# Back from the frequencies: the loads of the inverse transform in one run of 4 KB for each partition

## The chip, the cores and the metric

The kernel runs on one core of a Trainium2 chip. The metric is the device time of one execution, in microseconds; lower is better. The core has TensorE (PE) for matmuls, VectorE (DVE), ScalarE (ACT), GpSimd (POOL) and SyncE (SP), each with its own queue of instructions that it works through in order, and 16 DMA engines, which move data for all of them. In this kernel SP and ACT issue nearly all transfers, each on a queue of its own. SBUF is the memory of 128 partitions that the engines compute on, PSUM the one that TensorE writes, DRAM the large one outside.

## The reference

Two layers on an image `x` of 4 x 56 x 56 positions with 128 channels:

```
layer 0:  x = x + proj(7x7 neighbourhood attention(layernorm(x)))
          x = x + fc2(gelu(fc1(layernorm(x))))
layer 1:  t = x as 3136 tokens
          t = t + q * sum over tokens(k * v)              # of layernorm(t)
          t = t + gated mix of four STU branches          # of u = layernorm(t)
          branch i sees the first T/(1,2,4,8) tokens:
            U+ = irfft(rfft(phi) * rfft(u))               # 16 filters, causal
            U- = the same of u with every other sign turned
            out = U+ . M_phi_plus[i] + U- . M_phi_minus[i] + three lags of u . M_u[i]
```

The long convolution with its 16 filters is what the kernel does by transforms: tokens to frequencies, a 128 x 128 matrix product at every frequency, and frequencies back to tokens.

## The kernel before

All is float32. The program has four stages, one after the other.

1. Attention of the four images, with the dense work of the image before filled in between by a list of costs (`run`, `dense`). Its order is written out by hand.
2. The rest of the last image, while the matrices `M_phi` are weighted into `mc` (`matrices`). Its loads, `mat`, are 512 KB each: 128 partitions, one run of 4 KB in each.
3. The frequencies. There are R = 245 of them in each of two halves (`yd[0]` and `yd[1]`, sum and difference). `make` builds the matrices of eight frequencies at a time, `product` multiplies, and L1077 stores the result to `yd` in DRAM, which is laid out frequency x slot and token group x channel. A frequency has 128 rows of 128 channels, 64 KB.
4. The way back. The tokens are in four parts of N = 784 each, worked in two pairs (`pair`), and each part in L = 98 positions by eight phases. For each pair the odd half of the spectrum (`par` 1) gives the four odd phases, the even half (`par` 0) the four even ones. Since the frequencies stand on the partitions, 245 of them take two parts (`fh` 0 and 1): by `RT = (0, 128, R)` the first has 128 rows and the second 117.

What stage four does in turn, and on which engine:

- `fetch_back(pair, par, fh)` (L1088 to L1099) loads a part from `yd` to a tile of the ring on SP's queue. A row of the ring holds eight runs of 4 KB (a run is two token parts x four images x 128 channels), which in DRAM lie 8 KB apart, the other pair's between them. A load of 128 rows is one transfer. For 117 rows there are two: 112 rows, the largest multiple of 16, and 5 rows.
- `io` and `ie` (L1103, L1219) are the cosine and sine tables of the inverse transform, loaded on ACT's queue.
- `odd` and `even` are butterflies in place on VectorE (L1137, L1138).
- `products` runs the matmuls on TensorE (L1176): first all phases with `fh` 0, then all with `fh` 1, accumulating in eight PSUM banks. Then VectorE adds each bank to `xo` (L1188), the residual, which L1225 has loaded from `xd`: 98 partitions, four images of 4 KB in each. ACT's queue stores `xo` to the output (L1192).

The ring has two tiles, one for each `fh`, with room for both halves of the spectrum. A load for the second pair can begin when TensorE has read what stood there.

Stage three and four are ordered by the scheduler of the language, which reorders transfers on SP's queue by its own estimate. The order on SP's queue around the change is, before: first ring load (`par` 1, `fh` 0), two stores of `yd`, second ring load (`par` 0, `fh` 0), the last four stores of `yd`, then the second parts, `xo`, and the four loads of the second pair.

The inverse tables are computed on the host with zeros in the rows beyond 117, and `products` cuts the table to the rows of the data (`it[: z.shape[0]]`).

Of the kernel before, what the change touches and what calls it, by code (L numbers as in the profile page):

```python
# [9 lines left out]
FP = mybir.dt.float32  # L10
# [6 lines left out]
B, H, W, C = 4, 56, 56, 128  # L17
# [23 lines left out]
PH = 8  # L41
L = N // PH
R = NF // PH
RT = (0, 128, R)
SLOTS = (0, 6, 4, 2, 1, 7, 5, 3)
BACK = ((0, 2, 4, 6), (1, 5), (3, 7))
FC = 8
# [9 lines left out]
def conv_attn_hybrid_kernel(ctx: ExitStack, tc: tile.TileContext, a: dict, out: bass.AP):  # L57
    nc = tc.nc

    cpool = ctx.enter_context(tc.tile_pool(name="const", bufs=1))  # L60
    dram = ctx.enter_context(tc.tile_pool(name="scratch", bufs=1, space=DRAM))
    xd = dram.tile([B, T, C], FP, name="xd")
    ud = dram.tile([NP, B, C, NCH * CW], FP, name="ud")
    pd = dram.tile([2 * NK, NCH * CW], FP, name="pd")
    yd = dram.tile([2, R, C, C], FP, name="yd")

    front = ExitStack()
    fp = front.enter_context(tc.tile_pool(name="front", bufs=1))
# [895 lines left out]
    with tc.tile_pool(name="last", bufs=1, side="right") as own, tc.tile_pool(  # L964
        name="weigh", bufs=1, side="right"
# [14 lines left out]
    with tc.tile_pool(name="w3", bufs=2) as wp, tc.tile_pool(  # L980
        name="ps_g", bufs=6, space=PSUM
# [64 lines left out]
        def product(c, part):  # L1046

            v, g = spectra[c], made[c]
            f0 = part // 4 * 4
            h, last = part // 2 % 2, min(many[c], f0 + 4)  # L1050
            if part % 2 == 0:
                sums[0] = ps_y.tile([C, 4, C], FP, tag="y", name=f"py_{c}_{part}")
            py, f1 = sums[0], f0 + part % 2 * 2
            for f in range(f1, min(f1 + 2, last)):
                for r in range(2):
                    for m in range(4):
                        slot = SLOTS.index(4 * h + m)
                        nc.tensor.matmul(  # L1058
                            py[32 * m : 32 * m + 32, f - f0, :],
                            weights(v, 1 - r, f, slot),  # L1060
                            g[:, (2 * slot + r) * FC + f, :],
                            start=(r == 0),
                            stop=(r == 1),
                        )
            if part % 2 == 0:
                return

            k = last - f0
            if h == 0:
                sums[1] = wp.tile([C, 4, C], FP, tag="ya", name=f"ya_{c}_{part}", bufs=1)  # L1070
                nc.scalar.copy(sums[1][:, :k], py[:, :k])
                return
            for i, op in enumerate((ALU.add, ALU.subtract)):
                ys = wp.tile([C, 4, C], FP, tag=f"ys{i}", name=f"ys_{c}_{part}_{i}")
                nc.vector.tensor_tensor(ys[:, :k], sums[1][:, :k], py[:, :k], op)  # L1075
                at = FC * c + f0
                nc.sync.dma_start(yd[i, at : at + k].rearrange("f q e -> q f e"), ys[:, :k])  # L1077

# [1 line left out]
        PAIR = 2 * B * C  # L1082
# [3 lines left out]
            ring.append(gpool.tile([C, 2, 4, 2, PAIR], FP, tag="g", name=name))  # L1086

        def fetch_back(pair, par, fh):  # L1088
            f0, n = RT[fh], RT[fh + 1] - RT[fh]
            y = ring[fh][:, 1 - par]  # L1090
            for r0, r1 in ((0, n // 16 * 16), (n // 16 * 16, n)):
                if r0 < r1:
                    nc.sync.dma_start(
                        y[r0:r1].rearrange("f m s x -> f (m s) x"),
                        yd[par, f0 + r0 : f0 + r1].rearrange("f (k n) e -> f k (n e)", k=8)[
                            :, :, PAIR * pair : PAIR * (pair + 1)
                        ],
                    )
            return y[:n].rearrange("f m s (j x) -> f j m s x", j=2)  # L1099

        def odd_waves(pool, pair, fh):
            t = pool.tile([C, 32 * L], FP, tag="io", name=f"io_{pair}_{fh}")
# [27 lines left out]
    with tc.tile_pool(name="w4", bufs=1) as wp, tc.tile_pool(  # L1130
        name="ps_t", bufs=8, space=PSUM
# [34 lines left out]
        def products(pair, phases, terms, xos, dst):  # L1166


            banks = {}
            for fh in range(2):  # L1170
                for j, p, *what in phases:
                    if fh == 0:
                        banks[j, p] = ps_t.tile([L, B, C], FP, tag="t", name=f"pi_{pair}_{j}_{p}")
                    of = terms(fh, j, *what)
                    for k, (it, z) in enumerate(of):
                        nc.tensor.matmul(  # L1176
                            banks[j, p],
                            it[: z.shape[0]],
                            z,
                            start=(fh == 0 and k == 0),  # L1180
                            stop=(fh == 1 and k == len(of) - 1),
                        )
                    yield
                    if fh == 0:
                        continue
                    xo = xos[j][:, :, p, :]
                    o = 2 * pair + j
                    nc.vector.scalar_tensor_tensor(  # L1188
                        xo, banks[j, p], on[:L, o : o + 1], xo, ALU.mult, ALU.add
                    )  # L1190
                    if dst and p == 6:
                        nc.scalar.dma_start(dst[j], xos[j].rearrange("n b p e -> n b (p e)"))  # L1192
# [6 lines left out]
        for pair in range(2):  # L1199
            here, into = (  # L1200
                [
                    d[:, N * o : N * (o + 1)].rearrange("b (n p) e -> n b (p e)", p=PH)
                    for o in (2 * pair, 2 * pair + 1)
                ]
                for d in (xd, tokens_out)
            )
            ys, xos = {}, []
            ios = [
                waves_back[0] if pair == 0 else odd_waves(wpool, pair, 0),
                odd_waves(wp, pair, 1),  # L1210
            ]
            ys[1, 0] = fetch_back(pair, 1, 0) if pair else ready[1]
            ys[1, 1] = fetch_back(pair, 1, 1)
            ies = []

            def even_loads():
                for fh in range(2):
                    t = wp.tile([C, 16 * L], FP, tag=f"ie{fh}", name=f"ie_{pair}_{fh}")
                    nc.scalar.dma_start(t, a["itab_even"][pair, fh])  # L1219
                    ies.append(t.rearrange("f (j p r n) -> f j p r n", j=2, p=4, r=2))  # L1220
                ys[0, 0] = fetch_back(pair, 0, 0) if pair else ready[0]
                ys[0, 1] = fetch_back(pair, 0, 1)
                for j in range(2):
                    xo = wp.tile([L, B, PH, C], FP, tag=f"xo{j}", name=f"xo_{pair}_{j}")
                    nc.sync.dma_start(xo.rearrange("n b p e -> n b (p e)"), here[j])  # L1225
                    xos.append(xo)

            if pair == 0:
                even_loads()
            for par, step, phases in ((1, odd, odd_phases), (0, even, even_phases)):  # L1230
                zs = {}
                for fh in range(2):
                    for j in range(2):
                        zs[fh, j] = step(ys[par, fh][:, j])
                        for _ in range(4):
                            next(behind, None)
                for _ in behind:
                    pass
                if par and pair:
                    even_loads()  # L1240

                def terms(fh, j, *what, zs=zs, ios=ios, ies=ies):
                    if len(what) > 1:
                        kind, i = what
                        return [
                            (ios[fh][:, j, kind, m, r, i], zs[fh, j][kind][2 * m + r])
                            for m in range(2)
                            for r in range(2)
                        ]
                    return [(ies[fh][:, j, what[0], r], zs[fh, j][what[0]][r]) for r in range(2)]  # L1250

                behind = products(pair, phases, terms, xos, None if par else into)
# [7 lines left out]
def _laid_out(inputs):  # L1260
# [8 lines left out]
    x = a["x"].reshape(B, NG, GR, NQ, QC, C)  # L1269
    a["x"] = x.transpose(0, 5, 1, 3, 2, 4).reshape(B, C, NG, GT)  # L1270

    r, c, kr, kc = np.ix_(range(GR), range(QC), range(KR), range(KC))
    i, j = kr - r, kc - c
    inside = (i >= 0) & (i < WIN) & (j >= 0) & (j < WIN)
    at = np.where(inside, i * WIN + j, 0)
# [39 lines left out]
    for name, kinds, m in (("itab_even", BACK[:1], 1), ("itab_odd", BACK[1:], 2)):  # L1315
        inv = np.zeros((NP // 2, 2, C, 2, len(kinds), m, 2, len(kinds[0]), L))
        for k, ps in enumerate(kinds):

            of = both[:, :, ps, :, :m].reshape(NP // 2, 2, L, len(ps), 2, m, R)
            for i in range(2):  # L1320
                part = of[..., RT[i] : RT[i + 1]].transpose(0, 6, 1, 5, 4, 3, 2)
                if m == 1:
                    part = part.transpose(0, 1, 2, 3, 5, 4, 6).reshape(
                        NP // 2, -1, 2, 1, 2, len(ps), L
                    )
                inv[:, i, : part.shape[1], :, k] = part
        a[name] = inv.reshape(NP // 2, 2, C, -1).astype(np.float32)

    turn = 2 * np.pi / PH * np.outer(np.arange(PH), SLOTS)
# [29 lines left out]
```

## Time and profile before

| | us |
|---|---|
| median of 3 runs | 2086.72 (2086.64 to 2090.88) |
| the profiled execution's own time | 2095.97 |
| its span, first to last instruction | 2094.2 |
| TensorE busy over the span | 1896.0 (91%) |
| VectorE, ScalarE, GpSimd busy | 1230.1, 1000.9, 854.7 |
| way back, first ring load issued to the end of the span | 1857.9 to 2094.2 |
| TensorE busy from 1858 to 2094 | 183.4 of 236.0 |
| ring loads | 8 of 4096 or 3584 KB, 4 of 160 KB |
| `xo` loads, `out` stores | 4 each, 1568 KB |
| `io`, `ie` loads | 4 of 1568 KB, 4 of 784 KB |

The profile shows one execution. In a line of a group or of the timeline, `128*98 128x512` is a matmul whose weights have 128 rows and 98 columns and whose output is 512 wide; `x64` counts instructions. A float32 matmul of the program is two instructions here. `issue` is time in which an engine waited for nothing that the profile shows. Start times are from the span's start.

### The profile page before, as it was taken

The page shows a single profiled execution, that of the slowest core. Times are in us where ns is not written, and L with a number is a line of the kernel's source. Part 1 is how long each engine was busy: PE and PEld are TensorE (multiplying, and loading weights), DVE is VectorE, ACT ScalarE, POOL GpSimd, SP SyncE. Part 2 cuts the span into 40 slices and gives each one's busy share as a digit, 9 for nine tenths or more (in the row PEclk, how much of TensorE's full clock was granted, in tenths as well). Part 3 has the DMA queues.
Part 4 walks back from the last instruction along what each step waited for, and adds up shares of the span by engine and source line. Part 5 has one row for each costly group of instructions (what it writes and reads, how often), then busy time and mean ns, then how long its engine had stood idle before and what let it go on. Part 6 is the DMA issues. An engine that isn't in the chain of part 4 may idle for free.

```text
span 2094.2 us, 56418 instructions
## 1 busy us (share of the span) xinstructions
PE 1896.0 (91%) x23878; PEld 1201.0 (57%) x23878; DVE 1230.1 (59%) x2636; ACT 1000.9 (48%) x2199; POOL 854.7 (41%) x1272
## 2 busy tenths in 40 slices
PE   6899999998998989999999876999999999978896
PEld 3565554564554654554654334888888888852332
DVE  3777545555445555445655742677766766655566
ACT  2466675554675555765553331555555555530000
POOL 2233222462122562113740151777777777730000
PEclk8899999998999999999999986999999999988998
DMA  3130000242000450000445364344444444369993
GB/s 109 35 122 11 1 1 1 94 152 93 1 1 1 141 172 25 1 1 14 165 160 168 114 227 120 104 129 129 124 120 129 129 124 124 98 224 270 229 276 100
DMA packets 189989, 221.95 MB, mean 106 GB/s; under 512 B 10964, under 2 KB 170005, under 8 KB 187144
## 3 DMA queue, kind: packets, MB, share of 16 engines
q1 hardware_dynamic: 181596, 165.24, 28.0%
q0 software_dynamic: 2752, 34.33, 4.2%
q10 hardware_dynamic: 5388, 18.76, 2.8%
q8 instruction: 188, 3.08, 0.6%
q14 instruction: 65, 0.53, 0.1%
HBM read 140.33 MB, written 77.97 MB: 104 GB/s over the span
## 4 chain that ended last, share of the span: by engine, by line
PE 68%; DMA 9%; issue 7%; DVE 5%; ACT 4%; SPq 3%; POOL 2%; another core or an unknown queue 0%; ACTq 0%; DVEq 0%; POOLq 0%
PE pg L1027 14%; PE py L1058 12%; PE ppt L761 5%; PE px L658 4%; PE ph L511 3%; DMA xo<-xd 3%; PE pf L502 3%; PE pl L710 3%; PE pi L1176 3%; PE par L602 2%; DMA ring<-yd 2%; PE pav L807 2%; PE pv L788 2%; DMA tab<-in_tab 2%; ACT p L737 2%
## 5 line engine op out<-in xcount | busy, mean ns | idle before, releaser
L750 POOL TENSOR_SCALAR p<-p,den 112x280 f32<-112x280 f32 x448 | 216.2, 503 | 558.9 <-DVE den L748 291.7
L1040 DVE COPY g<-pg 128x512 f32<-128x512 f32 x496 | 320.1, 689 | 186.8 <-PE pg L1027 186.8
L1038 ACT COPY g<-pg 128x512 f32<-128x512 f32 x496 | 271.1, 602 | 263.9 <-PE pg L1027 263.9
L1027 PE MATMUL pg<-ph,mc 32*128 32x128 f32 x7936 | 308.1, 288 | 26.8 <-DMA ph<-pd 15.5
L1027 PEld LDWEIGHTS pg<-ph,mc 32*128 32x128 f32 x7936 | 257.5, 190 | 70.4 <-issue 57.8
L737 ACT ACTIVATE p<-p,low 112x280 f32<-112x280 f32 x448 | 231.2, 517 | 135.5 <-DVE low L723 134.7
L1058 PE MATMUL py<-g,v 128*32 128x128 f32 x7840 | 277.8, 281 | 7.0 <-issue 5.9
L1058 PEld LDWEIGHTS py<-g,v 128*32 128x32 f32 x7840 | 220.3, 152 | 37.9 <-issue 7.8
L723 DVE CUSTOM_DVE_ANT_0 p<-pl,bias 112x280 f32<-112x280 f32 x448 | 174.3, 443 | 3.2 <-PE pl L710 2.7
L761 PEld LDWEIGHTS ppt<-ident,p 112*120 112x120 f32 (+1 forms) x1344 | 138.3, 126 | 53.1 <-issue 40.4
L761 PE MATMUL ppt<-ident,p 112*120 112x112 f32 (+1 forms) x1344 | 154.9, 263 | 1.8 <-POOL p L750 1.0
L658 PE MATMUL px<-tab,tok 98*128 98x496 f32 x256 | 124.8, 628 | 23.1 <-DMA tab<-in_tab 14.9
L1176 PE MATMUL pi<-ring,io 128*98 128x512 f32 (+1 forms) x256 | 118.0, 624 | 29.5 <-DVE ys L1075 10.9
L666 POOL TENSOR_TENSOR ab<-ab,w 128x496 f32<-128x496 f32 x60 | 74.3, 1238 | 125.0 <-ACT w L665 124.9
L774 DVE COPY middle<-ppt 40x448 f32<-40x448 f32 x112 | 68.3, 610 | 95.1 <-PE ppt L761 94.8
L511 PE MATMUL ph<-ln_m,w_fc 128*128 128x448 f32 x224 | 111.6, 593 | 4.0 <-DVE ln_m L492 4.0
L519 ACT ACTIVATE h<-ph,b_fc 128x448 f32<-128x448 f32 x112 | 69.4, 633 | 71.6 <-PE ph L511 71.3
L1176 PEld LDWEIGHTS pi<-ring,io 128*98 128x98 f32 (+1 forms) x256 | 44.1, 174 | 103.1 <-issue 80.1
L1137 DVE TENSOR_TENSOR ring<-ring 128x1024 f32<-128x1024 f32 (+5 forms) x48 | 56.8, 1219 | 76.0 <-DMA ring<-yd 76.0
L502 PE MATMUL pf<-h,w_fc 128*128 128x448 f32 x224 | 101.0, 541 | 0.0
L710 PE MATMUL pl<-kt,qt 32*112 32x280 f32 x896 | 91.0, 442 | 9.7 <-ACT qt L468 5.1
L658 PEld LDWEIGHTS px<-tab,tok 98*128 98x128 f32 x256 | 48.7, 204 | 81.0 <-issue 50.6
(225 smaller groups left out, 3122.0 us busy)
## 6 DMA issues: line engine op xcount, KB each, us to landing
ud<-ab POOLq DMA_DIRECT2D x16, 1984.0 KB, 7.0
yd<-ys SPq DMA_DIRECT2D x122, 256.0 KB
xc<-ud SPq DMA_DIRECT2D x30, 1024.0 KB
tab<-in_tab SPq DMA_DIRECT2D x160, 189.9 KB
ring<-yd SPq DMA_DIRECT2D x4, 4096.0 KB
ring<-yd SPq DMA_DIRECT2D x4, 3584.0 KB
mat<-in_M_phi_plus SPq DMA_DIRECT2D x16, 512.0 KB
mat<-in_M_phi_minus SPq DMA_DIRECT2D x16, 512.0 KB
```

The lines of the kernel that those rows point to most:

```text
L502: nc.tensor.matmul(po[:, :GT], late["w_fc2"][:, i, :], hts[g - 1][i], start=(i == 0), stop=(i == 3),)
L511: nc.tensor.matmul(ph[:, :GT], w_fc1[:, i * C : (i + 1) * C], lnm[:, g * GT : (g + 1) * GT], start=True, stop=True,)
L658: nc.tensor.matmul(ps, toks[i // 4][:, i % 4, :], next(tab), start=True, stop=True)
L723: nc.vector.tensor_tensor_reduce(out=f["p"][:, h, :], in0=f["pls"][h][:TQ, :KEYS], in1=bias[:, h, :], scale=-1.0, scalar=3.0e38, op0=ALU.a ...
L737: nc.scalar.activation(f["p"][:, h, :], f["p"][:, h, :], AF.Exp, bias=f["low"][:, h : h + 1], scale=-1.0, accum_out=f["den"][:, h : h + 1],)
L750: nc.gpsimd.tensor_scalar(f["p"][:, h, :], f["p"][:, h, :], f["den"][:, h : h + 1], 1.0, ALU.mult, ALU.mult)
L761: nc.tensor.transpose(ppt[:nk, h * TQ : (h + 1) * TQ], f["p"][:, h, KC * KAT[c] : KC * KAT[c] + nk], ident[:TQ, :TQ],)
L1027: nc.tensor.matmul(banks[rg][:, q, :], mc[r, 4 * u + q, :], t[r, at : at + CW], start=True, stop=True,)
L1038: nc.scalar.copy(into, src)
L1040: nc.vector.tensor_copy(into, src)
L1058: nc.tensor.matmul(py[32 * m : 32 * m + 32, f - f0, :], weights(v, 1 - r, f, slot), g[:, (2 * slot + r) * FC + f, :], start=(r == 0), stop ...
L1176: nc.tensor.matmul(banks[j, p], it[: z.shape[0]], z, start=(fh == 0 and k == 0), stop=(fh == 1 and k == len(of) - 1),)
```

## The change

`yd` gets 136 rows of 128 channels for each frequency instead of 128; the last eight are never written or read. A frequency's rows thus lie 68 KB apart instead of 64.

`RT` becomes `(0, 117)`: a list of first rows, not of bounds. Both parts have 128 rows, and the second begins at 117, so rows 117 to 127 are loaded twice. The host puts zeros in the first 11 rows of the second part's tables, so that they don't count twice.

`fetch_back` issues eight transfers in place of one or two, each with one run of 4 KB for every one of 128 partitions. The `xo` load becomes four transfers, one for each image. The stores of `yd` write the same bytes to the new rows.

```diff
-RT = (0, 128, R)
+RT = (0, R - C)
...
-    yd = dram.tile([2, R, C, C], FP, name="yd")
+    yd = dram.tile([2, R, C + 8, C], FP, name="yd")
...
-                nc.sync.dma_start(yd[i, at : at + k].rearrange("f q e -> q f e"), ys[:, :k])
+                nc.sync.dma_start(yd[i, at : at + k, :C].rearrange("f q e -> q f e"), ys[:, :k])
...
         def fetch_back(pair, par, fh):
-            f0, n = RT[fh], RT[fh + 1] - RT[fh]
             y = ring[fh][:, 1 - par]
-            for r0, r1 in ((0, n // 16 * 16), (n // 16 * 16, n)):
-                if r0 < r1:
+            for m in range(4):
+                for r in range(2):
+                    row = 16 * (2 * m + r) + 8 * pair
                     nc.sync.dma_start(
-                        y[r0:r1].rearrange("f m s x -> f (m s) x"),
-                        yd[par, f0 + r0 : f0 + r1].rearrange("f (k n) e -> f k (n e)", k=8)[
-                            :, :, PAIR * pair : PAIR * (pair + 1)
-                        ],
+                        y[:, m, r],
+                        yd[par, RT[fh] : RT[fh] + C, row : row + 8].rearrange("f n e -> f (n e)"),
                     )
-            return y[:n].rearrange("f m s (j x) -> f j m s x", j=2)
+            return y.rearrange("f m s (j x) -> f j m s x", j=2)
...
-                            it[: z.shape[0]],
+                            it,
...
-                    nc.sync.dma_start(xo.rearrange("n b p e -> n b (p e)"), here[j])
+                    for b in range(B):
+                        nc.sync.dma_start(
+                            xo[:, b].rearrange("n p e -> n (p e)"), here[j][:, b]
+                        )
...
-                part = of[..., RT[i] : RT[i + 1]].transpose(0, 6, 1, 5, 4, 3, 2)
+                part = of[..., RT[i] : RT[i] + C].transpose(0, 6, 1, 5, 4, 3, 2).copy()
+                part[:, : i * (C - RT[1])] = 0
...
-                inv[:, i, : part.shape[1], :, k] = part
+                inv[:, i, :, :, k] = part
```

In the list of the built program's instructions, SP's queue goes from 12 ring loads and 4 `xo` loads to 64 and 16. All 16 transfers of the first two ring loads but one stand between the two pairs of `yd` stores: first transfer, two stores, fifteen transfers, the last four stores. After these come one transfer of the even second part, the eight of the odd one and the other seven of the even one. The numbers of matmuls and of VectorE's operations are the same.

## The prediction

> **What bounds the kernel now.** I read the slices of the page first, then TensorE's timeline of the last stage, then who waited there, then the transfer rates stretch by stretch.
>
> The change touches only the last stage, the way back, so the question is what ends last there. In the slices (40 of 52 us each), DMA is busiest in that stage alone:
>
> ```profile
> DMA  3130000242000450000445364344444444369993
> GB/s 109 35 122 11 1 1 1 94 152 93 1 1 1 141 172 25 1 1 14 165 160 168 114 227 120 104 129 129 124 120 129 129 124 124 98 224 270 229 276 100
> ```
>
> Three slices at 9 tenths or more, yet at 229 to 276 GB/s. Next, TensorE's timeline of the stage (start, length, then in brackets the idle time before and what ended it):
>
> ```profile
> 1878.93 30.47 PE L1176 MATMUL pi<-ring,io 128*98 128x512 f32 x64 [10.93 <-DVE ys L1075]
> 1919.56 2.03 PE L1176 MATMUL pi<-ring,io 117*98 117x512 f32 x2 [10.16 <-DVE ring L1137]
> 1921.83 28.66 PE L1176 MATMUL pi<-ring,io 117*98 117x512 f32 x62 [0.24 <-DVE ring L1138]
> 1952.68 29.42 PE L1176 MATMUL pi<-ring,ie 128*98 128x512 f32 x64 [2.19 <-DVE xo L1188]
> 1990.31 56.89 PE L1176 MATMUL pi<-ring,io 128*98 128x512 f32 x128 [8.21 <-DVE ring L1138]
> 2055.27 4.47 PE L1176 MATMUL pi<-ring,ie 128*98 128x512 f32 x6 [8.07 <-DVE xo L1188]
> 2060.01 25.14 PE L1176 MATMUL pi<-ring,ie 128*98 128x512 f32 x58 [0.26 <-DVE xo L1188]
> ```
>
> From 1878.93 TensorE works 177.1 us and stands idle 29.1 us (10.16 + 0.24 + 2.19 + 8.21 + 8.07 + 0.26). It ends at 2085.2; the end of the span, 2094.2, is the last addition and the last store, 9.0 us on. The idle time is blamed on VectorE, but VectorE itself waits for the loads:
>
> ```profile
> DVE ring L1137 <- DMA ring<-yd: 76.0, 8, 16.0
> DVE xo L1188 <- DMA xo<-xd: 2.5, 1, 2.5
> ```
>
> So the stage is bound by its loads, with TensorE 29 us behind as the next bound. Then the rates (stretch, its length, busy us of PE, weight load, DVE, ACT, POOL, granted clock, DMA share, GB/s):
>
> ```profile
> 1096.00:1103.00 7.00, 3.64 (x17) 0.80 (x15) 6.62 (x3) 3.56 (x6) 0.00 (x0) 0.99 1.01 397
> 1858.00:1876.00 18.00, 6.28 (x160) 5.20 (x160) 2.54 (x6) 0.86 (x2) 0.00 (x0) 0.67 1.00 382
> 1891.00:1895.00 4.00, 4.00 (x10) 1.49 (x9) 4.00 (x3) 0.00 (x0) 0.00 (x0) 1.00 1.05 231
> 1926.00:1951.00 25.00, 24.50 (x58) 9.11 (x56) 8.15 (x5) 0.00 (x0) 0.00 (x0) 1.00 1.04 208
> 1963.00:1975.00 12.00, 12.00 (x29) 4.61 (x28) 7.77 (x12) 0.00 (x0) 0.00 (x0) 1.00 1.03 207
> ```
>
> The engines are full in all five, at either 400 or 207 GB/s. The first is not this stage: it is the queue of `mat` loads (L948), 512 KB each, 128 partitions with one run of 4 KB. The second is the first ring load (128 rows, eight runs each). The third is the first load of 112 rows; from there on the rate is halved, through the `xo` loads of 98 partitions, and in the fifth even for a ring load of 128 rows. Nothing shows why.
>
> **What the Trainium skill says.** "DMA: Bandwidth & Descriptors", Why a DMA increments its semaphore by 16: the number of DMA engines is the largest up to 16 that divides the slowest dimension of both sides. So 112 rows take 16 engines with 7 rows each, 5 rows take 5 engines, 98 take 14. No view shows engines; the halving begins with the first transfer that isn't of 128 rows, which fits. The same page, Latency and other measured facts: row pitches of large powers of two slow copies, and 4 KiB of padding restored the full rate. It names pitches from 512 KiB; at 64 KB the trace has 382 GB/s once and 207 later, so pitch alone isn't the cause. The same page, Rules for kernel authors, wants transfers of 1 MiB and more; against that stand the 397 GB/s of 512 KB loads above. "TensorE: Matmul & The Clock Gate", LDWEIGHTS: the time goes by columns, not by rows. The trace agrees, here and for the matmul (mean ns behind the busy time):
>
> ```profile
> L1176 PEld LDWEIGHTS pi<-ring,io 128*98 128x98 f32 x128 | 22.3, 176 | 56.3 <-issue 46.1 <-DVE ring L1138 9.3 <-DVE ring L1137 0.6
> L1176 PEld LDWEIGHTS pi<-ring,io 117*98 117x98 f32 x128 | 21.7, 172 | 46.8 <-issue 34.0 <-DVE ring L1137 11.0 <-DVE ring L1138 1.9
> L1137 DVE TENSOR_TENSOR ring<-ring 128x1024 f32<-128x1024 f32 x12 | 14.4, 1220 | 25.2 <-DMA ring<-yd 25.2
> L1137 DVE TENSOR_TENSOR ring<-ring 117x1024 f32<-117x1024 f32 x12 | 14.3, 1219 | 17.6 <-DMA ring<-yd 17.6
> ```
>
> **The change part by part.**
>
> Compute with 128 rows instead of 117: 1219 to 1220 ns for VectorE, and the matmuls differ by less than their clock does. Nothing.
>
> Bytes: 11 rows of 32 KB for four loads, 1.44 MB: 3.6 us of engine time at 400 GB/s, 7 us at 207. But before, engines 0 to 4 had 7 rows and the eight runs of a sixth row from the 5-row transfer, 64 runs in all; after, every engine has 8 rows, 64 runs. The engine that lands last carries no more. Nothing on the path.
>
> Issues: 12 ring loads become 64 and 4 `xo` loads 16, so 64 more on SP's queue. The `mat` loads follow each other on it in 0.4 to 0.6 us, and 512 KB last 1.3 us at 400 GB/s: hidden. Bare, it would be 64 x 0.5 = 32 us. In the built program each transfer waits for the one that had its semaphore before; there are eight, shared by SP and ACT. So about 4 MB are outstanding, 10 us at 400 GB/s, against about 4 us from issue to use (first `mat` issue at 1090.55, used at 1094.77). Hidden too.
>
> The stores to `yd` (L1077) keep their 512-byte runs; their rows lie 4 KB further apart. They are stage three's, where `py` and `pg` on TensorE bound. Nothing.
>
> A new wait: the second part now begins at row 117 and ends at 244, so all its transfers wait for the last stores of `yd`, which stand behind the second ring load in SP's queue; before, only 5 rows did. Second load over at about 1887.5 (before, VectorE had it at 1889.19 with those stores in front), stores 1.5 us, 1 us to hear of it: issue at 1890 where the 112 rows were issued at 1886.28. Behind it on SP stand all later loads.
>
> Now the timeline. First ring load unchanged, TensorE starts at 1879 and is through the first 64 at 1909.4. The second odd part: in SP's queue one even transfer and eight odd (4.7 MB), beside them `io` 1.6 and `ie` 1.6 MB; 7.9 MB at 400 GB/s are 20 us, with 3 us to land: 1913. VectorE takes 1.3 us to the first product (1918.28 to 1919.56 before): 1914.3. Idle 5.1 with the 0.24, where it was 10.4. At 300 GB/s, the rate of `io` mixed with ring now, it would be 26 us and nothing gained here; I take the middle, 8 us.
>
> From 1917 TensorE has work to 1977 (30.7 + 29.4). To arrive by then minus VectorE's 5: the rest of the even part 3.7 MB, `io` 1.6, `xo` 3.2 at 200 GB/s (still 98 partitions), next odd load 4.2 and another `io` 1.6. At 400 that is 9 + 4 + 16 + 10.5 + 4 = 44 us from 1916: 1960, 12 us early. The later loads each have 28 us of TensorE for 4.2 MB and a table. So 2.19, 8.21 and 8.33 of idle time go: 18.7. With 2.4 from the first gap, 21; less about 1 for gaps where load and table meet: **20 us**. The profiled execution's span becomes 2074. That execution took 2095.97 where the median is 2086.72; the difference is taken off the whole: **2067 us**.
>
> **The rivals.**
>
> *Part of the loads stay at half rate.* The fifth stretch speaks for it: 128 rows at 207 GB/s. `xo` still uses 14 engines, so two run ahead. If ring loads of the even part and of pair one average 300 GB/s, the first gap stays 10 and about 10 us of the others go: 2077.
>
> *Nothing changes.* The half rate belongs to the stage, not to the shape. Then 39.6 MB after 1890 at 238 GB/s, what the stage from 1889 to 2055 has now, against 38.2: 6 us, less what the even share of engines saves. 2084 to 2091.
>
> *Slower: the pitch of 68 KB.* The first loads are fast at 64 KB now; at 68 KB they may not be. If every ring load has 207 GB/s from 1860 on: ring 33.6 and `xo` 6.4 MB take 193 us, tables 9.6 MB at 300 another 32: last `xo` at 2085 instead of 2058, 27 us on, and that path goes on to the end: 2114. It decides once ring and `xo` average under about 240 GB/s, where that sum gives 2058 again. For it: nothing in the trace has this pitch. Against it: `mat` at its 16 KB pitch.
>
> **How the numbers follow.** Full rate 0.50 (2059 to 2075), part 0.16, nothing 0.12, slower 0.22. A measurement of this kernel tells 0.2%, some 4 us, from no change: faster 0.64, same 0.10, slower 0.26, as a third of the "nothing" case lies above the bound. The range leaves out the half of the slower case beyond 2100 and the best beyond full cover (all 29 us gone: 2058): 2056 to 2100. Likeliest case alone: 2059 to 2075.
>
> **What would show it.** Right: rates near 400 in the stretches of ring loads after 1890, VectorE's wait for `ring<-yd` falling from 76 us to under 40, TensorE without a gap over 2 us after 1920. Wrong: 207 GB/s in the ring stretches, or the first ring load landing later than 1876 (pitch), or SP waiting for transfers while the DMA share is below 0.9 (the eight semaphores).

## The result, and the profile after

The changed kernel takes 2052.95 us (median of four, 2051.11 to 2057.71) against 2086.68 us (2083.28 to 2090.88) of the kernel before beside it: a ratio of 0.984, interval 0.982 to 0.987. The forecast was 2067 us in a range of 2056 to 2100: the sign was right, the gain of 20 us too small by 14, and the time lies below the range.

The page's slices of the changed kernel, as in the prediction:

```profile
DMA  3130000243000243000354535444444444439991
GB/s 111 36 124 12 1 1 1 81 165 100 1 1 1 94 152 100 1 1 1 106 182 144 189 118 188 112 132 126 127 123 125 117 132 121 125 86 349 361 343 65
```

Again three slices in which DMA is full, now at 343 to 361 GB/s where it was 229 to 276, and the last slice is nearly empty. TensorE's timeline of way back:

```profile
1871.68 29.98 PE L1176 MATMUL pi<-ring,io 128*98 128x512 f32 x64 [14.29 <-DVE ring L1138]
1902.54 28.26 PE L1176 MATMUL pi<-ring,io 128*98 128x512 f32 x64 [0.88 <-DVE ring L1137]
1930.64 27.63 PE L1176 MATMUL pi<-ring,ie 128*98 128x512 f32 x64
1958.11 55.10 PE L1176 MATMUL pi<-ring,io 128*98 128x512 f32 x128
2013.04 27.63 PE L1176 MATMUL pi<-ring,ie 128*98 128x512 f32 x64
```

After its first product TensorE waits once, for 0.88 us, where it waited for 29.1. And there is a second difference: the same 384 passes (a pass is one of the two instructions of a product) take 168.6 us, the sum of the second column, where they took 177.1. Who waited:

```profile
DVE ring L1137 <- DMA ring<-yd: 25.8, 6, 7.3
DVE ring L1137 <- DMA xo<-xd: 2.6, 1, 2.6
PE pi L1176 <- DVE ring L1137: 0.9, 1, 0.9
```

VectorE's 76.0 us of waiting for ring loads are 25.8. The rates, with the columns of the prediction's stretches:

```profile
1881.00:1901.00 20.00, 20.00 (x48) 7.65 (x47) 15.32 (x15) 0.00 (x0) 0.00 (x0) 1.00 1.02 416
1916.00:1928.00 12.00, 12.00 (x29) 4.62 (x28) 11.98 (x10) 0.00 (x0) 0.00 (x0) 1.00 1.00 256
1931.00:1942.00 11.00, 11.00 (x27) 4.29 (x26) 8.63 (x12) 0.00 (x0) 0.00 (x0) 1.00 1.02 412
1958.00:1970.00 12.00, 12.00 (x29) 4.62 (x28) 12.00 (x13) 0.00 (x0) 0.00 (x0) 1.00 1.01 401
```

Ring loads move at 401 to 416 GB/s, mixed with `io` and `ie` too (the first stretch). Only the `xo` loads, still of 98 partitions, are slow (second stretch), and what comes behind them is fast again. In the kernel before the rate came back once as well, late: from 2003 to 2021 us, with the second load of 128 rows of pair 1 beside `out` stores and a table, its trace has 368 GB/s, which the prediction's "from there on the rate is halved" leaves out.

One measure makes the rest readable. In the profiles of this case the work ahead of way back shifts from one to the next: its first load is issued anywhere between 1844 and 1861 us. What follows repeats: from that issue to the end of the span, three profiles of the changed kernel have 202.5, 203.0 and 202.4 us. Before it was 236.3, in the one profile that there is. I call this time the tail. It is 33.8 us shorter, as the medians are. Its parts, before and after: to TensorE's first product 21.1 and 24.1, from there to its last 206.2 and 169.0, behind it 9.0 and 9.4.

### The profile page after: what moved, and what is told of

It reads as the page before. It is cut to its first block, busy times and chain, and to the rows that moved or that the text cites. A ratio compares the mean times of both kernels' runs of the same rounds, so it can differ in the third digit from the quotient of the medians.

```text
span 2050.1 us, 56526 instructions
## 1 busy us (share of the span) xinstructions
PE 1884.5 (92%) x23878; PEld 1196.7 (58%) x23878; DVE 1230.8 (60%) x2636; ACT 1001.1 (49%) x2199; POOL 853.6 (42%) x1272
## 4 chain that ended last, share of the span: by engine, by line
PE 75%; issue 7%; DMA 6%; DVE 5%; ACT 4%; SPq 1%; POOL 1%; ACTq 0%; POOLq 0%; DVEq 0%
PE pg L1028 14%; PE py L1059 12%; PE pi L1176 7%; PE px L659 5%; PE ppt L762 5%; PE ph L512 3%; PE pl L711 3%; PE pf L503 3%; PE par L603 3%; PE pav L808 2%; PE pv L789 2%; DMA ring<-yd 2%; DMA tab<-in_tab 2%; ACT p L738 2%; PE pk L450 2%
## 5 line engine op out<-in xcount | busy, mean ns | idle before, releaser
L1176 PE MATMUL pi<-ring,io 128*98 128x512 f32 x256 | 113.3, 603 | 15.2 <-DVE ring L1138 14.3
L659 PEld LDWEIGHTS px<-tab,tok 98*128 98x128 f32 x256 | 49.3, 207 | 79.2 <-issue 51.3
L525 DVE SCALAR_TENSOR_TENSOR x<-pf,b_fc,x 128x448 f32<-128x448 f32 x28 | 19.1, 683 | 124.2 <-PE pf L503 124.2
L1176 PEld LDWEIGHTS pi<-ring,io 128*98 128x98 f32 x256 | 42.7, 168 | 85.3 <-issue 80.7
```

The lines of the kernel that those rows point to most:

```text
L659: nc.tensor.matmul(ps, toks[i // 4][:, i % 4, :], next(tab), start=True, stop=True)
L1176: nc.tensor.matmul(banks[j, p], it, z, start=(fh == 0 and k == 0), stop=(fh == 1 and k == len(of) - 1),)
```

## The experiments

The change has four parts: rows (128 and 128 instead of 128, 112 and 5), runs (eight transfers instead of one), pitch (68 KB instead of 64), and the four transfers of `xo`. My theory was that the rows gave the rate. The runs on this question, in us; a ratio is to the kernel before, run beside them, with its 95% interval:

| kernel | median | ratio | tail | TensorE, first to last product |
|---|---|---|---|---|
| before | 2086.68 | | 236.3 | 206.2 |
| changed | 2052.95 | 0.984 (0.982 to 0.987) | 202.5 | 169.0 |
| changed, 64 KB | 2050.16 | 0.984 (0.980 to 0.987) | 202.4 | 169.3 |
| changed, `xo` whole | 2050.84 | 0.983 (0.980 to 0.987) | 201.9 | 169.9 |
| changed, one transfer for a part | 2066.70 | 0.990 (0.987 to 0.993) | 216.8 | 187.8 |
| changed, 128, 112 and 5 rows | 2070.53 | 0.992 (0.989 to 0.995) | 223.4 | 191.0 |
| before, 128 rows alone | 2058.59 | 0.985 (0.983 to 0.988) | 207.3 | 175.1 |
| before, eight transfers alone | 2074.99 | 0.992 (0.989 to 0.995) | 214.1 | 181.5 |
| changed, halves of 64 rows | 2108.84 | 1.008 (1.006 to 1.010) | 249.5 | 209.4 |

The kernel before took 2086.88 us beside the third to the sixth row and 2093.87 us beside the last three, so rows are compared by ratio and tail.

### Pitch and `xo`: nothing

```diff
-    yd = dram.tile([2, R, C + 8, C], FP, name="yd")
+    yd = dram.tile([2, R, C, C], FP, name="yd")
```

> The changed kernel with the rows of yd 64 KB apart again, all else kept. My theory (rows: what halved the rate of the loads was their shape, 112 and 5 of 128 partitions, not the pitch): no change, 2050 to 2056 us, runs of 4 KB at 159 to 170 ns, TensorE idle under 2 us after its first product. Rival (pitch: rows 64 KB apart meet in the same part of DRAM): 2072 to 2088 us, runs at 300 ns or more and the gaps of the kernel before back (up to 33 us).

Measured 2050.16 us, tail 202.4. The pitch does nothing, neither for good nor for bad.

```diff
-                    for b in range(B):
-                        nc.sync.dma_start(
-                            xo[:, b].rearrange("n p e -> n (p e)"), here[j][:, b]
-                        )
+                    nc.sync.dma_start(xo.rearrange("n b p e -> n b (p e)"), here[j])
```

> The changed kernel with each xo as one transfer of four runs for every one of 98 partitions again. Rows: xo moves at 200 to 260 GB/s in both forms and is not waited for; the next pair's first load is behind it in the queue with some 20 us of slack: 2049 to 2058 us. Rival (runs): four runs for one partition let two engines skip ahead, and the loads of the next pair behind xo stay at 300 ns or more: 2060 to 2075 us.

Measured 2050.84 us, tail 201.9. Nothing either. Rows and runs are left.

### Rows given back

```diff
-RT = (0, R - C)
+RT = (0, 128, R)
...
+            for r0, r1 in ((0, n // 16 * 16), (n // 16 * 16, n)):
```

(each run stays its own transfer; the tables' zeros and the cut of the table go back with it)

> The changed kernel with the frequencies split 128 and 117 again (117 as 112 and 5 rows), each run its own transfer; 68 KB and xo kept. Rows: the second part's loads halve the rate, 300 ns or more per run from the first of them on, TensorE's gaps come back with their restarts: 2072 to 2088 us. Rival (runs): no change, 2049 to 2057 us. Rival (pitch): no change either.

Measured 2070.53 us. The rates of three stretches in which transfers of 112 rows are under way:

```profile
1880.00:1886.00 6.00, 6.00 (x15) 2.31 (x14) 6.00 (x4) 0.00 (x0) 0.00 (x0) 1.00 1.04 246
1910.00:1924.00 14.00, 8.61 (x13) 2.90 (x14) 9.17 (x8) 0.00 (x0) 0.00 (x0) 0.60 1.02 239
1962.00:1970.00 8.00, 8.00 (x20) 3.01 (x19) 7.05 (x7) 0.00 (x0) 0.00 (x0) 1.00 1.04 257
```

112 rows move at 239 to 257 GB/s with single runs and at 68 KB too; a run of 4 KB takes some 270 ns in the trace where it takes 159 to 165 in a transfer of 128 rows. That is the theory's sign, but the time lies just below what I had put down: against the two runs above, made beside it, some 20 us are lost, more than half of the gain but not all of it.

### Rows alone, and runs alone

```diff
-RT = (0, 128, R)
+RT = (0, R - C)
...
+            for h in range(2):
+                nc.sync.dma_start(
+                    y[:, 2 * h : 2 * h + 2].rearrange("f m s x -> f (m s) x"),
```

> The kernel before with one part of the change alone: both parts of the frequencies with 128 rows. Rows stay 64 KB apart, each xo one transfer, and each load of a part is two transfers of four runs for every one of the 128 partitions, with which VectorE's order stays the old one (second odd part ahead of second even part). Rows (the shape with 128 partitions is what gives the rate): as the changed kernel, 2049 to 2057 us, one gap of TensorE of about 2 us or less after its first product, runs of 4 KB at 159 to 170 ns outside the loads of xo. Rival (one run for each descriptor list, that is eight transfers, is needed too): 2062 us or more, with loads behind xo at 300 ns.

(the tables' zeros go with it; a part is loaded in two transfers of four runs, since one transfer of eight changes the order, as the next run shows)

Measured 0.985 of the kernel before: at the table's 2086.68 that is 2056 us. Ring loads move at 404 to 420 GB/s, ahead of `xo` and behind it:

```profile
1900.00:1904.00 4.00, 2.75 (x7) 0.82 (x5) 0.00 (x0) 0.00 (x0) 0.00 (x0) 1.00 1.03 420
1946.00:1956.00 10.00, 10.00 (x24) 3.79 (x23) 5.01 (x5) 0.00 (x0) 0.00 (x0) 1.00 1.01 406
1960.00:1970.00 10.00, 10.00 (x25) 3.84 (x24) 10.00 (x12) 0.00 (x0) 0.00 (x0) 1.00 1.02 404
```

So the rows bring 29.0 of the tail's 33.8 us without the other parts. I had expected one gap of 2 us or less; it has 5.53:

```profile
1872.50 30.24 PE L1174 MATMUL pi<-ring,io 128*98 128x512 f32 x64 [13.25 <-DVE ring L1136]
1908.28 29.44 PE L1174 MATMUL pi<-ring,io 128*98 128x512 f32 x64 [5.53 <-DVE ring L1135]
```

Most of the difference is the order on SP's queue. The scheduler puts the first transfer of the even second part ahead of the odd one, for which TensorE waits. Here that transfer has 2048 KB, in the changed kernel 512: 1.57 MB more ahead of what is needed, 3.9 us at 404 GB/s. The odd second part lands 57.8 us behind the first ring issue, in the changed kernel 52.7; the order explains 3.9 of these 5.1 us, and what the rest is stays open.

```diff
-                    nc.sync.dma_start(
-                        y[:, m, r],
-                        yd[par, RT[fh] : RT[fh] + C, row : row + 8].rearrange("f n e -> f (n e)"),
-                    )
+            nc.sync.dma_start(
+                y.rearrange("f m s x -> f (m s) x"),
+                yd[par, RT[fh] : RT[fh] + C, :C].rearrange("f (k n) e -> f k (n e)", k=8)[
+                    :, :, PAIR * pair : PAIR * (pair + 1)
+                ],
+            )
```

> The changed kernel with each load of a part as one transfer of eight runs for every one of the 128 partitions instead of eight transfers; 128 rows, 68 KB and the loads of xo kept. Rows: no change, 2050 to 2056 us. Rival (runs: a transfer with several runs for one partition lets the queue's engines drift apart and keeps the rate down once it has fallen, as the 128-row load of pair 1 did before, 207 GB/s): the loads ahead of the first xo keep 400 GB/s, those behind xo fall to about 300 ns per run; TensorE then gets gaps of about 8 us in pair 1, each with a restart of its clock: 2062 to 2078 us.

Measured 2066.70 us, within the rival's range, and yet the rival is wrong. Ahead of `xo` and behind it the rate is full:

```profile
1896.00:1904.00 8.00, 4.58 (x11) 1.49 (x9) 3.75 (x4) 0.00 (x0) 0.00 (x0) 0.92 1.02 410
1970.00:1976.00 6.00, 6.00 (x15) 2.31 (x14) 6.00 (x8) 0.00 (x0) 0.00 (x0) 1.00 1.02 413
```

TensorE's one long gap is not in pair 1 but ahead of the odd second part, as its timeline shows:

```profile
1870.41 30.17 PE L1174 MATMUL pi<-ring,io 128*98 128x512 f32 x64 [10.12 <-DVE ys L1076]
1917.52 2.03 PE L1174 MATMUL pi<-ring,io 128*98 128x512 f32 x2 [16.94 <-DVE ring L1135]
1919.79 28.54 PE L1174 MATMUL pi<-ring,io 128*98 128x512 f32 x62 [0.25 <-DVE ring L1136]
```

The timeline of VectorE says why:

```profile
1901.97 4.49 DVE L1135 TENSOR_TENSOR ring<-ring 128x2048 f32<-128x2048 f32 x2 [4.25 <-DMA ring<-yd]
1906.38 4.49 DVE L1136 SCALAR_TENSOR_TENSOR ring<-ring 128x2048 f32<-128x2048 f32 x2
...
1916.24 2.36 DVE L1135 TENSOR_TENSOR ring<-ring 128x1024 f32<-128x1024 f32 x2 [2.50 <-DMA ring<-yd]
```

The wide butterflies (2048) are the even second part's, and they come at 1902, ahead of the odd ones (1024) at 1916. With one transfer for a part, the scheduler puts the whole even second part first, on SP's queue and on VectorE, and the odd part lands 65.8 us behind the first ring issue, 13 later than in the changed kernel. This run lost to an order, not to a rate. It also had 128 rows with eight runs in one transfer at 413 GB/s behind `xo`; the kernel before had 207 for such a load.

```diff
-                        y[r0:r1].rearrange("f m s x -> f (m s) x"),
+                                y[r0:r1, m, r],
```

(in the kernel before, with two loops over `m` and `r` around it)

> The kernel before with each run its own transfer and nothing else: 128, 112 and 5 rows, 64 KB. Rows: the second parts still come at about 270 ns a run and 250 GB/s, since 112 rows remain; the loads of 128 rows behind xo come back to 160 ns sooner than before: 2066 to 2080 us. Rival (eight transfers are what gives the rate): 2049 to 2057 us.

Measured 0.992 of the kernel before, at the table's 2086.68 that is 2069 us. The stretches of a 112-row load, and of a 128-row load behind `xo`:

```profile
1924.00:1932.00 8.00, 7.75 (x14) 2.47 (x13) 4.92 (x5) 0.00 (x0) 0.00 (x0) 0.74 1.03 265
1998.00:2004.00 6.00, 6.00 (x15) 2.31 (x14) 6.00 (x6) 0.00 (x0) 0.00 (x0) 1.00 1.03 412
```

The 112 rows stay slow, 128 rows behind them are fast again, and that is enough to close the gaps of pair 1; the gap of 10.6 us ahead of the odd second part stays. So rows and runs each do a good part alone, and their gains don't add: the loads need only keep ahead of TensorE. The low rate that stayed on in the kernel before, for a load of 128 rows too, needed both 112 rows and eight runs in a transfer: without either it is gone. In its trace the first 128-row load of pair 1 ends on its first engine at 1953.1 and on its last at 1986.7, 33.6 us apart; in the run with one transfer of 128 rows for each part it is 5.8 us. That engines this far apart keep each other slow fits, but no run shows it by itself.

### Why rows: halves of 64

```diff
-                    nc.sync.dma_start(
-                        y[:, m, r],
-                        yd[par, RT[fh] : RT[fh] + C, row : row + 8].rearrange("f n e -> f (n e)"),
-                    )
+                    for h in (0, 64):
+                        nc.sync.dma_start(
+                            y[h : h + 64, m, r],
+                            yd[par, RT[fh] + h : RT[fh] + h + 64, row : row + 8].rearrange(
+                                "f n e -> f (n e)"
+                            ),
+                        )
```

> The changed kernel with each transfer of 128 rows cut into two of 64 rows (partitions 0 to 63, then 64 to 127): the same runs of 4 KB, the same 64 descriptors of data for each engine and part, twice the transfers. If the rate hangs on the 16 engines writing to different ports of SBUF[...]: about twice the time of a run, 270 to 330 ns and 200 to 250 GB/s in the loads ahead of xo too, TensorE's start late by 8 us or more and its gaps back: 2085 to 2115 us. Rival (only the number of runs for each engine, or a number of rows that 16 divides evenly into fours, matters): 160 to 170 ns and 2050 to 2060 us.

Measured 1.008 of the kernel before: the only form of the loads that is slower. The stretch of the first two ring loads, the fast ones in all other kernels, and one behind:

```profile
1868.00:1886.00 18.00, 1.21 (x20) 0.68 (x16) 3.91 (x7) 0.28 (x1) 0.00 (x0) 0.50 1.04 236
1935.00:1955.00 20.00, 13.71 (x27) 5.01 (x28) 9.17 (x8) 0.00 (x0) 0.00 (x0) 0.74 1.04 237
```

The same runs of 4 KB now take about 286 ns, at full DMA share. The size of a transfer isn't the reason: a later run has transfers of 128 rows and the same 256 KB, at 391 to 396 GB/s (below). The Trainium skill has a reason, on "SBUF — State Buffer", Door 1: The DMA port swizzle: partitions 0 to 63 reach 8 of the 16 ports on SBUF's DMA side, with some 218 GB/s as their limit. The same page, "Can I just issue two DMAs to hit both halves?", has two transfers to the two halves together gain 6% on one. That makes 231 GB/s as an estimate; measured 236. And "DMA: Bandwidth & Descriptors", The descriptor swizzle, says that with 128 partitions each engine writes to a port of its own. For 112 or 98 partitions neither page says where engines meet. That they meet at ports is argued from the halves; measured is 239 to 265 GB/s for 112 rows. Another reading of the halves is left: a transfer of 64 rows has four runs for each of 16 engines where one of 128 has eight, and no run changes that number with the partitions kept. So it is shown that 128 rows in one transfer give the rate, and open why fewer don't.

### The clock behind a gap

The work that shrank from 177.1 to 168.6 us is a matter of TensorE's clock. Stretches of the kernel before behind three of its gaps (length, PE busy, granted clock, DMA share, GB/s):

```profile
1919.00:1925.00 6.00, 5.19 (x6) 0.50 0.98 269
1952.70:1957.00 4.30, 4.30 (x6) 0.60 1.09 291
1990.30:1995.00 4.70, 4.69 (x7) 0.63 1.03 235
```

and of the changed kernel at its start and behind its only gap:

```profile
1871.60:1876.00 4.40, 4.32 (x5) 0.50 1.03 387
1902.50:1907.00 4.50, 4.39 (x9) 1.00 1.04 420
```

Behind each such gap the passes come 0.85 us apart for 3.5 to 6 us, instead of 0.43; I call this a restart. The Trainium skill, "TensorE: Matmul & The Clock Gate", What's actually happening, says that an array idle for about 3.4 us works at half its clock until it has been busy for about as long. The trace agrees on the half clock and roughly on its length, but not on the idle time: the second stretch stands behind a gap of 2.19 us. There are five restarts before and one after. At full clock 64 passes take 27.63 us and 128 take 55.10. The groups behind the five restarts are 11.5 us longer than that in all, the one behind the changed kernel's 2.4, and 0.6 are lost at full clock behind its gap of 0.88 us: 8.5 in sum.

Does this price reach the end? I filled the gaps of the kernel before with products of zeros:

```diff
+                    if (j, p) == phases[0][:2]:
+                        for _ in range(WARM.get((pair, p % 2, fh), 0)):
+                            nc.tensor.matmul(
+                                banks[j, p], idle[:, :L], idle, start=(fh == 0), stop=(fh == 0)
+                            )
```

> The kernel before with TensorE kept busy for most of each of its later gaps: 10, 2, 7 and 7 products of a tile of zeros (128 x 98 by 128 x 512, two passes of 0.428 us each) are put ahead of the first product behind each gap; they add zero, or are overwritten. Loads, VectorE and the gaps' ends are as before. Theory (each gap of over some 2 us costs, beside its idle time, the restart of TensorE's clock: 2.4, 1.7, 1.8 and 2.2 us more for the first passes behind the four gaps of before): 2077 to 2082 us against 2086.7, and passes 0.43 us apart from the first one behind each gap. Rival (the slow passes are something else, or hidden): 2085 to 2089 us.

Measured 1.002 of the kernel before (1.0005 to 1.0042), tail 240.5: slower, where I expected 5 to 10 us less.

```profile
1909.45 8.75 PE L1176 MATMUL pi<-idle 128*98 128x512 f32 x20
1919.46 1.96 PE L1181 MATMUL pi<-ring,io 117*98 117x512 f32 x4 [1.26 <-DVE ring L1137]
1921.73 25.99 PE L1181 MATMUL pi<-ring,io 117*98 117x512 f32 x60 [0.31 <-DVE ring L1138]
...
1989.32 55.10 PE L1181 MATMUL pi<-ring,io 128*98 128x512 f32 x128
2054.88 8.25 PE L1176 MATMUL pi<-idle 128*98 128x512 f32 x14 [10.47 <-DVE xo L1193]
2062.97 27.63 PE L1181 MATMUL pi<-ring,ie 128*98 128x512 f32 x64
```

The mechanism is shown: with the clock kept up, 64 passes take 27.95 us where they took 30.69, and 128 take 55.10 where they took 56.89. The gain isn't: the gaps end when loads land, so TensorE waits the longer. And the last zeros stood in the wrong place: TensorE waited there for a bank that VectorE frees, the zeros waited with it and then took 8.25 us. Where they begin, this run was 1.6 us ahead of the kernel before, counted from the first ring load. Up to there it was to save 5.9 us (2.4, 1.7 and 1.8), so most of what restarts cost was hidden behind the loads. What the fourth would have brought isn't shown.

In the changed kernel I expected another answer, for there hardly a load is waited for. The first try had its products wait:

```diff
+                        for _ in range(15):
+                            nc.tensor.matmul(banks[j, p], idle[:, :L], idle, start=True, stop=True)
```

> The changed kernel with 15 products of a tile of zeros (two passes of 0.428 us each, 12.8 us) put ahead of the first product of way back, in the 14.3 us that TensorE waits there; their results are overwritten. Theory (the first five slow passes, 2.2 us, are the restart of TensorE's clock, and with no gap left behind them nothing gives that time back to a load): the first 64 passes take 27.6 us instead of 29.8, and the kernel 1.5 to 2.5 us less than the changed kernel beside it. Rival (restarts are no cost): no change, 0.5 us either way.

```profile
1885.72 16.05 PE L1176 MATMUL pi<-idle 128*98 128x512 f32 x30 [20.38 <-POOL idle L1198]
1901.61 55.10 PE L1179 MATMUL pi<-ring,io 128*98 128x512 f32 x128
```

Measured 2077.69 us beside 2060.89 of the changed kernel. The zeros waited for GpSimd to write them (the memory was free only after the last store of `yd`), so it decides nothing on a restart. The second try used the odd waves, which are there:

```diff
+                        for _ in range(13):
+                            nc.tensor.matmul(
+                                banks[j, p], t[:, :L], t[:, : B * C], start=True, stop=True
+                            )
```

> The changed kernel with 13 products (26 passes, 11.1 us) of the odd waves with themselves ahead of the first product of way back; their data is there from the start, unlike the zeros tried before, and their results are overwritten. Theory (the slow first passes are the restart of TensorE's clock after a wait, and cost the end their full time where no load is waited for behind them): TensorE's 64 first passes take 27.4 to 28.2 us instead of 29.8, and the way from the first load to the end 200.3 to 201.5 us. Rival (a restart costs the end nothing): 202 to 203.5 us.

```profile
1866.37 13.19 PE L1177 MATMUL pi<-io 128*98 128x512 f32 x26 [0.85 <-DVE ys L1076]
1879.40 27.63 PE L1182 MATMUL pi<-ring,io 128*98 128x512 f32 x64
1911.21 29.28 PE L1182 MATMUL pi<-ring,io 128*98 128x512 f32 x64 [4.18 <-DVE ring L1137]
```

Measured 2061.59 us beside 2056.13, tail 204.7 against 202.4. The first 64 passes take 27.63 instead of 29.98, as the theory has it, and the gap ahead of the next grows to 4.18, with a restart there. The odd second part's landing decides when TensorE goes on, so my theory that this restart reaches the end falls as well. (VectorE also had that part 1.3 us later behind the first load than in the changed kernel beside it, 52.5 against 51.3; why is open.)

### Is there more to gain?

> The changed kernel itself once more, as the measure for the runs beside it: 2050 to 2060 us, or 0.981 to 0.987 of the kernel before.

> The changed kernel itself beside the next three. From the first load of way back to the end: 202 to 203.5 us as in its two profiles so far (202.5 and 203.0), of which 24 to TensorE's first product, 169 of TensorE, 9.4 behind.

The changed kernel, run again, had 2060.89 us (0.983, 0.980 to 0.985) and 2056.13 us (0.981, 0.978 to 0.984). Four versions try to start TensorE sooner, the first two beside the 2060.89, the others beside the 2056.13. In the first the two odd loads of pair 0 are cut by order, first half first, and the even first part goes behind the last stores of `yd`; the second adds five products of zeros to it:

```diff
-                for par in (1, 0):
-                    ready[par] = fetch_back(0, par, 0)
+                ready[1] = fetch_back(0, 1, 0)
...
+            cut = 2 if par and not pair else 1
+            for j in range(cut):
...
+                        n, x = 8 // cut, PAIR // cut
+                        row = 16 * (2 * m + r) + 8 * pair + n * j
```

> The changed kernel, with what is left of waiting taken out of its start: the two odd loads of pair 0 as sixteen transfers of 2 KB runs, the first of the two orders first, so that VectorE and TensorE begin on half the bytes (2 MB less at about 400 GB/s: 5 us, and VectorE's first butterflies on one half: some 2 us), and the even first part behind the last stores of yd and the odd second part. Theory (once the loads run at 400 GB/s, TensorE's start and its own 168 us set the end): TensorE starts 5 to 8 us sooner behind the first ring load and still has no gap over 2 us: 5 to 8 us less than the changed kernel beside it. Rival (runs of 2 KB move at a lower rate, or the second part of the even frequencies now comes too late): a gap of TensorE that takes the gain back, within 2 us of the changed kernel.

> Both: the odd loads first and in halves, and 5 products of zeros (4.3 us) in what is then left of TensorE's wait at the start. Theory: 6.5 to 10 us less than the changed kernel beside it. Rival: as far as the restart is no cost, no more than the loads' order alone gives.

Measured 2064.06 us and 2062.76 us, tails 204.4 and 204.3. In the first TensorE starts at +17.7 instead of +24.4 us, and later gaps take it back. The third cuts the odd loads but leaves the parts' order alone; a fourth adds five products of the odd waves to it:

> The changed kernel with the two odd loads of pair 0 as sixteen transfers of 2 KB runs each, the first order's half first; SP's order between the parts kept (first even part ahead of the last stores of yd, as in the changed kernel). Theory (TensorE's start is set by the landing of its first data, and the second odd part's first half comes as much sooner): start at +17 to +18 instead of +24 us behind the first load, a gap of 0 to 4 us ahead of the second part, 196 to 200 us from the first load to the end. Rival (the earlier start is given back in the gap ahead of the second part, whose load waits for the same stores of yd): a gap of 6 to 8 us and a restart, 202 to 204 us.

> Halves by order and 5 products (4.3 us) of the odd waves ahead of the first product. Theory: the gain of both, 194 to 199 us from the first load to the end. Rival (the gap ahead of the second part takes it all): 202 to 204 us.

Measured 2058.69 us and 2056.86 us, tails 202.6 and 202.3. The third's timeline:

```profile
1879.78 29.28 PE L1178 MATMUL pi<-ring,io 128*98 128x512 f32 x64 [7.94 <-DMA ring<-yd]
1909.65 28.37 PE L1178 MATMUL pi<-ring,io 128*98 128x512 f32 x64 [0.59 <-DVE ring L1139]
1937.86 1.88 PE L1178 MATMUL pi<-ring,ie 128*98 128x512 f32 x4
1942.03 3.68 PE L1178 MATMUL pi<-ring,ie 128*98 128x512 f32 x8 [2.29 <-DVE xo L1190]
```

TensorE starts at +18.4 us, the gap ahead of the odd second part is 0.59, so the odd part did come sooner, against the rival. But then TensorE waits for banks, which `xo` additions free on VectorE, where they stand behind the even butterflies, and these waited for their loads. Its loads show that runs of 2 KB in transfers of 256 KB keep the rate:

```profile
1868.00:1876.00 8.00, 2.17 (x41) 1.36 (x40) 2.88 (x5) 0.27 (x1) 0.00 (x0) 0.58 1.07 391
1876.00:1880.00 4.00, 0.22 (x1) 0.25 (x2) 3.53 (x4) 0.00 (x0) 0.00 (x0) 0.50 1.06 396
```

No version beats the changed kernel by what can be measured. After the change loads, VectorE's order and TensorE stand within a few us of each other, and 6 us taken from one come back in another.

## Why the prediction was wrong in size

The steps that failed are three sizes in the sum: TensorE's work, taken as 177.1 us where it fell to 168.6; the first gap, put at 8 us where 0.88 were left; and TensorE's start, taken as unchanged where it came 3.0 us later. The first two hid more gain than the third took, and the time fell below the range.

Its mechanism held: loads bound the stage, the shape of the transfers held them back, and TensorE was next. All three signs named for it are there: over 400 GB/s in the ring stretches, VectorE's wait at 25.8 us, no gap over 2 us behind 1920. Step by step:

- **128 rows cost no compute time, 64 more issues and 1.44 MB are hidden.** Right: the 320 passes behind the gap take 138.6 us, 0.43 each, and the loads keep ahead of them.
- **The pitch.** Costed at nothing, right (tail 202.4 and 202.5). The slower rival built on it had 0.22; at either pitch the rate is the same.
- **The new wait for the last stores.** The second parts were to be issued 32.1 us behind the first ring load; it was 31.3. From 1876 to 1881 us it leaves the DMA engines at a share of 0.47.
- **The rates before.** They were read as "either 400 or 207 GB/s"; the third stretch has 231. The "nothing changes" rival takes 238 GB/s from 1889 to 2055, where the trace has 248; its 6 us stay 6.
- **TensorE's start: failed.** It was taken over as unchanged, 21.1 us behind the first load; it was 24.1. VectorE began 18.1 us behind that load in both kernels, but in the changed one three additions and two subtractions stand ahead of the first product, where one of each did.
- **The first gap: failed.** I worked out 5.1 us for 400 GB/s and took "the middle, 8 us" towards 300, because `io` mixed with ring had 300 before. Mixed they run at 416 now: the 300 was the old shape's. The gap is 0.88. Of the 7.1 us between, 3.0 are no gain, since TensorE's later start took them from the gap. 4.1 are left.
- **The later gaps vanish, 18.7 us.** Right. The 1 us set aside for loads and tables that meet wasn't needed.
- **TensorE's work: failed, and the larger term.** The sum took 177.1 us as fixed and removed idle time alone. The slow passes behind the gaps were in view (`x2` in 2.03 us, `x6` in 4.47), and the skill's page on the clock gate was cited for weights only. With the gaps four of five restarts went: 8.5 us.

The 20 us forecast, with 4.1, 8.5 and 1 added and 0.4 for a longer end taken off, are 33.2; measured 33.8. (Of the rest 0.5 is no time: where the changed kernel's groups follow without a gap, their lengths overlap by 0.16 us each.) The low end of the range came from the same error: "all 29 us gone: 2058" was called the best case, but without gaps TensorE's time is below that. The 8.5 us belong to the gaps, though: the two runs that took restarts away and left the loads as they were gained nothing at the end.

## What to carry to other kernels

When a stage's gaps close, count what stands behind each gap too: TensorE's first 4 to 6 us at half clock belong to the gap's price, but only for a change that removes the gap; keeping the clock up inside a wait for loads gained nothing in the two runs here. Load all 128 partitions in every transfer, some rows twice if need be: 11 rows more on 117 bought 1.6 times the rate here. And cut transfers small enough that what the queue's order puts ahead of the needed data is short: at the same rate, one transfer in place of eight cost some 14 us.

## What the runs showed of the hardware that I had not expected

- 128 rows in two transfers of 64: 236 GB/s, against 401 to 416 in one. 112 rows: 239 to 265. 98 partitions: 256.
- 512 KB and 256 KB transfers of 128 rows, queued one behind another, keep 391 to 416 GB/s, like those of 2 and 4 MB (404 to 420).
- A gap of 0.88 us left TensorE's clock up, and one of 1.26; one of 4.18 brought a restart. The 3.4 us of the skill's page are no sharp bound here, and at about 2.3 and at 3.2 us both occur. 2.19 in the kernel before brought one (clock 0.60 behind it), 2.41 in the third profile of the changed kernel did not (clock 1.00, and its next 64 passes took 28.26 us, as behind 0.88). 3.21 in the version with the even part behind the stores brought one (clock 0.50), 3.23 in the run with 112 and 5 rows did not at once (clock 1.00 over its next six passes).
